# FP4 weights of the last block: transposing the block scales alone and rounding the values in the transposed layout

## The chip, the cores and the metric

The kernel runs on one core of a Trainium2 chip. The metric is the device time of one launch in microseconds, the median of several runs. TensorE is PE in the profile (its weight loads PEld), VectorE is DVE, ScalarE ACT, GpSimd POOL, and SyncE, which issues every DMA of this kernel, SP.

## The reference

A network of two gated blocks on x (8 batches of 224 rows, width 512), each made of a cross-attention to a context of 750 rows and a feed-forward part, both added with a tanh gate. Attention 0 has 16 heads of 32, attention 1 has 8 heads of 64 and a mask; feed-forward 0 is ternary with a depthwise convolution; feed-forward 1 is FP4. Only this last part matters here:

```python
def fp4_quant_dequant(x):            # BLOCK = 16, along the last dim
    xb = x.reshape(shape[:-1] + (shape[-1] // BLOCK, BLOCK))
    scale = jnp.max(jnp.abs(xb), axis=-1, keepdims=True) / 6.0
    scale = jnp.maximum(scale, jnp.float32(1e-12))
    xn = xb / scale
    idx = jnp.searchsorted(_MID, jnp.abs(xn))
    q = _GRID[idx] * jnp.sign(xn) * scale

def fp4_linear(x, w):
    return jnp.einsum('bsk,nk->bsn', fp4_quant_dequant(x), fp4_quant_dequant(w))

gate = fp4_linear(x, w_gate)
y = fp4_linear(x, w_up)
return fp4_linear(jax.nn.silu(gate) * y, w_down)
```

w_gate and w_up are 1408 x 512, w_down is 512 x 1408. A block is 16 neighbours along the contracted dimension, so a scale belongs to one output row and 16 inputs. TensorE wants the weights with the contracted dimension on the partitions, which is the transposed layout: there a block lies across 16 partitions.

## The kernel before, in words

The program is written as generators. Each yields pairs (PE us, DVE us) after handing out a few instructions; these are hints of cost, and the planner interleaves the generators by them. The order in which PE, DVE and ACT instructions are handed out is the order in which each engine runs them (`pin`). The order of SP and POOL is set when the program is built, by when each instruction is thought to be ready; each of them then works strictly in order.

There are 16 rounds of attention, n = 0 to 15: `attention16` for the 8 batches of block 0, then `attention8` (line 647 on) for those of block 1. A round of attention8 has 8 slots (4 head pairs, 2 row halves of 112). A slot does, on PE, the scores (L703), the product of the slot before with its values (L666), then other matmuls from queues, then the transposes of the softmax weights (L763). DVE adds the mask and takes the maximum (L720, L732), ACT takes the exponentials (L741) and copies the transposes out (L768). `fill` hands out matmuls of the queue (keys L312, queries L341, values L374, output projection L398) until a budget of PE us is spent; `pace` hands out steps of the list `beside` until a budget of DVE us is spent: 1.5 us ahead of the exponentials and 3.5 us in all by the second call in a slot. In slot 1 all values of the round are finished in one stretch (L374), and the next round's context is loaded (L293) once its buffer is free. L409 adds the output projection to x on DVE and so frees a bank of ps_m, of which there are two. L437, L439, L684 and L688 spread the softmax sums over the heads; they use the bank ps_t, of which there is one.

`last_weights` is the step in `beside` from round 8 on. It prepares the FP4 weights through `fp4_weights`, in 34 pieces of 128 rows by 512 (4 of them 384) columns: 11 of w_gate, 11 of w_up, 12 of w_down. For each piece:

- SP loads it (L1094, wraw), one piece ahead;
- `fp4_steps` finds the block maxima (L1061), the scale and its inverse (L1062, L1063), divides (L1066), rounds by adding and subtracting a power of two that is taken from the exponent (L1069, L1073 to L1075), and POOL multiplies by the scale again (L1076), in three steps with the hints 1.0, 1.1 and 1.6;
- one piece later PE transposes the 128 x 128 squares into ps_t (L1102, hint 0.45), four to a piece (three in a piece of 384), and ACT copies them to wg or wu (L1120), or to a buffer (L1130) from which SP writes them to the DRAM tensor wd_quantized (L1131).

Round 15 no longer has weights to prepare; its queue holds the first row tiles of feed-forward 1 (`ffn1_head`), which read wg and wu (L1168). After the attention `ffn1` runs the remaining tiles and loads wd once (L1316).

Of the kernel before, what the change touches and what calls it, by code (L numbers as in the profile page):

```python
# [63 lines left out]
class Net:  # L64
# [1014 lines left out]
    def fp4_weights(self, work, puts):  # L1079
# [5 lines left out]
            (put, src, r, c0, min(D, n_cols - c0))  # L1085
            for put, src, n_rows, n_cols in puts
# [4 lines left out]
        def load(n):  # L1091
            _, src, r, c0, width = pieces[n]
            raw = work.tile([128, D], F32, name="wraw", bufs=2)[:, :width]
            nc.sync.dma_start(out=raw, in_=src[r * 128 : (r + 1) * 128, c0 : c0 + width])  # L1094
            return raw

        def transposed(n, q):
            put, _, r, c0, width = pieces[n]
            nk = width // 128
            pt = self.ps("t", [128, nk, 128])  # L1100
            for k in range(nk):
                nc.tensor.transpose(pt[:, k, :], q[:, k * 128 : (k + 1) * 128], self.ident)  # L1102
            put(pt, c0 // 128, r)

        raw = load(0)
        for n in range(len(pieces)):
            ahead = load(n + 1) if n + 1 < len(pieces) else None
            q = work.tile([128, D], F32, name="wq4", bufs=2)[:, : pieces[n][-1]]
            yield from self.fp4_steps(work, q, raw, pieces[n][-1])
            if n:  # L1110
                transposed(n - 1, before)
                yield 0.45, 0
            raw, before = ahead, q
        transposed(len(pieces) - 1, q)

    def kept(self, dst):


        def put(pt, k, r):
            self.nc.scalar.copy(dst[:, k : k + pt.shape[1], r * 128 : (r + 1) * 128], pt)  # L1120

        return put

    def sent(self, work, dst):


        def put(pt, k, r):
            nk = pt.shape[1]
            some = work.tile([128, 4, 128], F32, name="wsome", bufs=2)
            self.nc.scalar.copy(some[:, :nk, :], pt)  # L1130
            self.nc.sync.dma_start(  # L1131
                out=dst[:, k : k + nk, r * 128 : (r + 1) * 128], in_=some[:, :nk, :]
            )

        return put
# [215 lines left out]
    def run(self):  # L1351
# [42 lines left out]
        def last_weights():  # L1394
# [5 lines left out]
            yield from self.fp4_weights(  # L1400
                self.ppool,
                (
                    (self.kept(self.wg), t["w_gate"], HID1, D),
# [153 lines left out]
```

## Time and profile before

| what | value |
|---|---|
| median of 3 runs | 2153.29 us (2151.72 to 2155.82) |
| the profiled execution, its own time | 2156.02 us |
| its span in the profile | 2154.2 us |
| first load of w_gate to last write of wd_quantized | 1171.6 to 1571.7 us |
| L1102, PE transposes of the weights | 132 of 273 ns |
| L1120 and L1130, copies to wg, wu and the send buffer | 34, of 585 ns (478 ns with 384 columns) |
| mean granted TensorE clock | 0.998 |

The time of a run is a little longer than the span, which is what the profiler saw of the engines. Times of single instructions below come from the profiled execution. A group of the profile is one line of the kernel on one engine: busy time, mean ns of one, then the idle time of the engine just ahead of it and what ended that. An instruction of PE is counted from its start to its modelled end; consecutive ones overlap, so what one costs in a row is read from the starts.

### The profile page before, as it was taken

The numbers are of one execution on the slowest core, as the hardware profiler recorded it, in microseconds if no ns is written. First come the engines' busy times: TensorE is split into PE (matmuls) and PEld (weight loads), VectorE is DVE, ScalarE is ACT, GpSimd is POOL, SyncE is SP. The second block draws the span as 40 slices with busy tenths as digits, with TensorE's granted clock in tenths as the row PEclk, the third lists the DMA queues.
The fourth block names the chain that finished last, engine by engine and source line by source line (L and its number), as shares of the span: only waits on it lengthen the run. The fifth ranks groups of instructions, "written<-read, shape, count | busy, mean of one in ns | idle before, by whom it ended". The sixth has DMA issues, their size and how long they took to land.

```text
span 2154.2 us, 32130 instructions
## 1 busy us (share of the span) xinstructions
PE 2107.8 (98%) x12606; PEld 1213.0 (56%) x12606; DVE 1362.9 (63%) x2795; ACT 1002.1 (47%) x2332; POOL 130.3 (6%) x146
## 2 busy tenths in 40 slices
PE   9999999999999999999999999999999999999999
PEld 5444545455554545455656575666656565665555
DVE  3776666677767676674456575654723467776665
ACT  3566667575767667573444343443534331111111
POOL 0000000000000000000000010111100001111111
PEclk9999999999999999999999999999999999999999
DMA  7200010100001010111011112112110011000000
GB/s 226 78 31 29 2 46 2 32 15 18 29 2 46 2 46 21 52 35 52 15 32 52 52 44 66 42 56 69 57 46 11 14 52 41 10 20 20 20 6 20
DMA packets 50215, 81.24 MB, mean 38 GB/s; under 512 B 3344, under 2 KB 29712, under 8 KB 49936
## 3 DMA queue, kind: packets, MB, share of 16 engines
q1 hardware_dynamic: 50064, 79.18, 11.7%
q8 instruction: 100, 1.64, 0.3%
q14 instruction: 51, 0.42, 0.1%
HBM read 65.28 MB, written 13.89 MB: 37 GB/s over the span
## 4 chain that ended last, share of the span: by engine, by line
PE 88%; DVE 5%; ACT 4%; issue 1%; DMA 0%; SPq 0%; POOL 0%; ACTq 0%; POOLq 0%; DVEq 0%
PE ps_m L374 15%; PE ps_m L312 13%; PE ps_big L1168 11%; PE ps_m L1200 6%; PE ps_pair L485 6%; PE ps_m L398 5%; PE ps_m L341 4%; PE ps_half L703 4%; PE ps_half L763 4%; PE ps_pa L666 4%; PE ps_pair L458 2%; ACT p L601 2%; PE ps_pa L576 2%; PE ps_t L907 2%; PE ps_m L1168 2%; PE ps_t L1021 1%
## 5 line engine op out<-in xcount | busy, mean ns | idle before, releaser
L502 ACT ACTIVATE p<-ps_pair,part 112x375 f32<-112x375 f32 x512 | 286.3, 571 | 192.0 <-DVE part L493 192.0
L312 PE MATMUL ps_m<-cx,wk 128*128 128x375 f32 x1024 | 370.5, 491 | 1.3 <-ACT kT L321 1.1
L374 PE MATMUL ps_m<-wv,cx 128*125 128x512 f32 x768 | 355.4, 602 | 0.0
L493 DVE TENSOR_REDUCE part<-ps_pair 112x2 f32<-112x750 f32 x256 | 228.2, 932 | 130.4 <-PE ps_pair L485 128.5
L312 PEld LDWEIGHTS ps_m<-cx,wk 128*128 128x128 f32 x1024 | 179.7, 191 | 118.0 <-issue 34.4
L374 PEld LDWEIGHTS ps_m<-wv,cx 128*125 128x125 f32 x768 | 135.5, 187 | 159.7 <-issue 158.0
L720 DVE CUSTOM_DVE_ANT_0 ps_half<-ps_half,mbias 112x750 f32<-112x750 f32 x128 | 121.1, 946 | 150.7 <-PE ps_half L703 150.0
L601 ACT ACTIVATE p<-ps_pair 125x896 f32<-125x896 f32 x192 | 165.0, 911 | 76.9 <-PE ps_pair L458 76.9
L485 PE MATMUL ps_pair<-kT,qT 32*112 32x375 f32 x1024 | 148.0, 522 | 0.2
L741 ACT ACTIVATE p<-ps_half,nm 112x750 f32<-112x750 f32 x128 | 113.4, 890 | 66.0 <-DVE nm L732 65.6
L1200 PE MATMUL ps_m<-wd,hqT 128*128 128x512 f32 x308 | 136.6, 592 | 0.0
L383 ACT COPY v<-ps_m 125x512 f32<-125x512 f32 x96 | 56.5, 589 | 152.2 <-PE ps_m L374 151.5
L935 DVE SCALAR_TENSOR_TENSOR y<-hp,cw,y 128x224 f32<-128x224 f32 x256 | 109.4, 448 | 20.2 <-ACT y L921 15.7
L398 PE MATMUL ps_m<-wo,aT 128*112 128x512 f32 x256 | 119.6, 602 | 0.0
L1179 ACT ACTIVATE gth<-ps_big 128x352 f32<-128x352 f32 x48 | 22.2, 463 | 206.9 <-PE ps_big L1168 206.9
L341 PE MATMUL ps_m<-xnT,wq 128*128 128x224 f32 x512 | 113.2, 360 | 0.6 <-ACT xnT L195 0.6
L1168 PE MATMUL ps_big<-wu,xqT 128*128 128x352 f32 x352 | 111.3, 459 | 0.0
L1168 PE MATMUL ps_big<-wg,xqT 128*128 128x352 f32 x352 | 111.3, 459 | 0.0
L768 ACT COPY p<-ps_half 125x672 f32<-125x672 f32 x128 | 85.9, 722 | 49.9 <-PE ps_half L763 49.7
L485 PEld LDWEIGHTS ps_pair<-kT,qT 32*112 32x112 f32 x1024 | 52.1, 170 | 98.7 <-ACT p L502 69.6
L502 ACT ACTIVATION_READ_ACCUMULATOR p<-ps_pair,part 112x1 f32 x512 | 103.5, 202 | 0.0
L763 PEld LDWEIGHTS ps_half<-ident,p 112*125 112x125 f32 x768 | 93.2, 189 | 16.1 <-issue 7.8
(223 smaller groups left out, 3026.4 us busy)
## 6 DMA issues: line engine op xcount, KB each, us to landing
cx<-in_ctx SPq DMA_DIRECT2D x32, 750.0 KB, 4.4
wst<-in_w SPq DMA_DIRECT2D x16, 512.0 KB, 8.1
x<-in_x SPq DMA_DIRECT2D x8, 448.0 KB, 6.0
mid<-x SPq DMA_DIRECT2D x8, 448.0 KB, 3.1
x<-mid SPq DMA_DIRECT2D x8, 448.0 KB, 3.5
last<-x SPq DMA_DIRECT2D x8, 448.0 KB, 3.1
out<-yout SPq DMA_DIRECT2D x14, 256.0 KB, 2.0
wraw<-in_w_gate SPq DMA_DIRECT2D x11, 256.0 KB, 2.6
```

The costliest lines, as they stand in the source:

```text
L312: nc.tensor.matmul(pk, lhsT=self.w["wk"][:, k, g * 128 : (g + 1) * 128], rhs=job["cx"][c][:, k, :], start=k == 0, stop=k == KC - 1,)
L341: nc.tensor.matmul(pq[:, g - g0, :], lhsT=self.w["wq"][:, k, g * 128 : (g + 1) * 128], rhs=xnT[:, k, :], start=k == 0, stop=k == KC - 1,)
L374: nc.tensor.matmul(pv, lhsT=job["cx"][c][:, k, at : at + CP], rhs=self.w["wv"][:, k, :], start=k == 0, stop=k == KC - 1,)
L398: nc.tensor.matmul(po, lhsT=aT[:, g, i * TP : (i + 1) * TP], rhs=self.w["wo"][:, g, :], start=g == 0, stop=g == KC - 1,)
L485: nc.tensor.matmul(sc[h // 2][:, h % 2, :MH], lhsT=qT[r, g, i * TP : (i + 1) * TP], rhs=kT[g][r, c * MH : (c + 1) * MH], start=True, stop= ...
L493: nc.vector.tensor_reduce(part[:, c, i, g, 2 * k : 2 * k + 2], sc[k][:, :, :MH], AX.X, ALU.max, negate=True)
L502: nc.scalar.activation(shown[:TP, h, :MH], sc[h // 2][:, h % 2, :MH], AF.Exp, bias=part[:, c, i, g, h : h + 1], accum_out=sums[:, c, i, g, ...
L601: nc.scalar.activation(p[:, 2 * k : 2 * k + 2, :], pw[k][:, :, : 2 * S], AF.Exp)
L720: nc.vector.tensor_tensor_reduce(out=src, in0=src, in1=masks[i], scale=1.0, scalar=-MASKED, op0=ALU.add, op1=ALU.max, accum_out=mx,)
L763: nc.tensor.transpose(pt[:, j // half, j % half * TP : (j % half + 1) * TP], p[:, h, j * CP : (j + 1) * CP], self.ident[:TP, :TP],)
L1168: nc.tensor.matmul(ps[:, :CW], lhsT=xqT[:, k, :], rhs=wt[:, k, c0 : c0 + CW], start=k == 0, stop=k == KC - 1,)
L1200: nc.tensor.matmul(po, lhsT=hqT[:, k, :], rhs=wd[:, k, :], start=k == 0, stop=k == NC1 - 1)
```

## The change

The values are no longer transposed on PE. The host hands in the three matrices in the transposed layout as well (w_gateT, w_upT, w_downT), beside the plain ones. The preparation has two passes for each matrix:

- `fp4_scales` (34 pieces as before) loads the plain piece, finds scale and inverse on DVE into one tile of 128 x 64 (wboth), transposes that tile with one PE instruction into ps_t, copies the 64 x 128 result to wrows (two buffers) on ACT, and writes it with two DMAs (scale, inverse; each from 32 partitions, 24 in a piece of 384) to a DRAM tensor, each row 16 times over, so that there every weight of the transposed layout has its own scale and inverse;
- `fp4_blocks` (35 pieces: 12 of w_gateT, 12 of w_upT, 11 of w_downT) loads a piece of the transposed matrix and the two pieces of scales and inverses that belong to it, divides and rounds on DVE with plain operands in place of broadcast ones, and POOL multiplies by the scale straight into wg or wu; for w_down it multiplies in place and SP writes the piece to wd_quantized.

The hints become 1.3 (scales), 0.1 for PE (its transpose), and 1.2 and 1.9 (values). wraw has three buffers instead of two. The order is: scales of w_gate, scales of w_up, values of w_gate, scales of w_down, values of w_up, values of w_down.

```diff
-    def fp4_weights(self, work, puts):
+    def fp4_scales(self, work, src, n_rows, n_cols, dst):
         nc = self.nc
         pieces = [
-            (put, src, r, c0, min(D, n_cols - c0))
-            for put, src, n_rows, n_cols in puts
+            (r, c0, min(D, n_cols - c0))
             for r in range(n_rows // 128)
             for c0 in range(0, n_cols, D)
         ]
         def load(n):
-            _, src, r, c0, width = pieces[n]
-            raw = work.tile([128, D], F32, name="wraw", bufs=2)[:, :width]
+            r, c0, width = pieces[n]
+            raw = work.tile([128, D], F32, name="wraw", bufs=3)[:, :width]
             nc.sync.dma_start(out=raw, in_=src[r * 128 : (r + 1) * 128, c0 : c0 + width])
             return raw
-        def transposed(n, q):
-            put, _, r, c0, width = pieces[n]
-            nk = width // 128
-            pt = self.ps("t", [128, nk, 128])
-            for k in range(nk):
-                nc.tensor.transpose(pt[:, k, :], q[:, k * 128 : (k + 1) * 128], self.ident)
-            put(pt, c0 // 128, r)
+        def sent(n, both):
+            r, c0, width = pieces[n]
+            nb = width // BLK
+            pt = self.ps("t", [2 * nb, 128])
+            nc.tensor.transpose(pt, both.rearrange("p a b -> p (a b)"), self.ident)
+            rows = work.tile([64, 128], F32, name="wrows", bufs=2)[: 2 * nb, :]
+            nc.scalar.copy(rows, pt)
+            for k in range(2):
+                nc.sync.dma_start(
+                    out=dst[k, c0 : c0 + width, r * 128 : (r + 1) * 128].rearrange(
+                        "(b j) n -> b j n", j=BLK
+                    ),
+                    in_=rows[k * nb : (k + 1) * nb, :].unsqueeze(1).to_broadcast([nb, BLK, 128]),
+                )
         raw = load(0)
-        for n in range(len(pieces)):
+        for n, (_, _, width) in enumerate(pieces):
             ahead = load(n + 1) if n + 1 < len(pieces) else None
-            q = work.tile([128, D], F32, name="wq4", bufs=2)[:, : pieces[n][-1]]
-            yield from self.fp4_steps(work, q, raw, pieces[n][-1])
+            nb = width // BLK
+            most = work.tile([128, D // BLK], F32, name="wmost", bufs=2)[:, :nb]
+            both = work.tile([128, 2 * D // BLK], F32, name="wboth", bufs=2)[:, : 2 * nb]
+            both = both.rearrange("p (a b) -> p a b", a=2)
+            nc.vector.tensor_reduce(
+                most, raw.rearrange("p (b k) -> p b k", k=BLK), AX.X, ALU.max,
+                apply_absolute_value=True,
+            )
+            nc.vector.tensor_scalar(both[:, 0, :], most, 1.0 / 6.0, 1e-12, ALU.mult, ALU.max)
+            nc.vector.reciprocal(both[:, 1, :], both[:, 0, :])
+            yield 0, 1.3
             if n:
-                transposed(n - 1, before)
-                yield 0.45, 0
-            raw, before = ahead, q
-        transposed(len(pieces) - 1, q)
-
-    def kept(self, dst):
-
-
-        def put(pt, k, r):
-            self.nc.scalar.copy(dst[:, k : k + pt.shape[1], r * 128 : (r + 1) * 128], pt)
-
-        return put
-
-    def sent(self, work, dst):
-
-
-        def put(pt, k, r):
-            nk = pt.shape[1]
-            some = work.tile([128, 4, 128], F32, name="wsome", bufs=2)
-            self.nc.scalar.copy(some[:, :nk, :], pt)
-            self.nc.sync.dma_start(
-                out=dst[:, k : k + nk, r * 128 : (r + 1) * 128], in_=some[:, :nk, :]
+                sent(n - 1, before)
+                yield 0.1, 0
+            raw, before = ahead, both
+        sent(len(pieces) - 1, both)
+        yield 0.1, 0
+
+    def fp4_blocks(self, work, src, scales, n_rows, n_cols, dst, kept):
+
+
+        nc = self.nc
+        pieces = [
+            (k, c0, min(D, n_cols - c0)) for k in range(n_rows // 128) for c0 in range(0, n_cols, D)
+        ]
+
+        def load(n):
+            k, c0, width = pieces[n]
+            rows, cols = slice(k * 128, (k + 1) * 128), slice(c0, c0 + width)
+            got = []
+            for name, ap in (
+                ("wraw", src[rows, cols]),
+                ("wscale", scales[0, rows, cols]),
+                ("winv", scales[1, rows, cols]),
+            ):
+                bufs = 3 if name == "wraw" else 2
+                got.append(work.tile([128, D], F32, name=name, bufs=bufs)[:, :width])
+                nc.sync.dma_start(out=got[-1], in_=ap)
+            return got
+
+        got = load(0)
+        for n, (k, c0, width) in enumerate(pieces):
+            ahead = load(n + 1) if n + 1 < len(pieces) else None
+            a, scale, e = got
+            nc.vector.scalar_tensor_tensor(a, a, DOWN, e, ALU.mult, ALU.mult)
+            nc.vector.tensor_scalar(
+                e.bitcast(I32), a.bitcast(I32), EXPONENT, None, ALU.bitwise_and
             )
-
-        return put
+            yield 0, 1.2
+            nc.vector.tensor_scalar(e, e, 1.0, STEP, ALU.max, ALU.mult)
+            nc.vector.tensor_tensor(a, a, e, ALU.add)
+            nc.vector.tensor_tensor(a, a, e, ALU.subtract)
+            where = dst[:, k, c0 : c0 + width]
+            nc.gpsimd.tensor_tensor(where if kept else a, a, scale, ALU.mult)
+            if not kept:
+                nc.sync.dma_start(out=where, in_=a)
+            yield 0, 1.9
+            got = ahead
     def ffn1_in(self, work, f, x, xn, xqT, bufs):
...
             self.wg = w1pool.tile([128, KC, HID1], F32, name="wg")
             self.wu = w1pool.tile([128, KC, HID1], F32, name="wu")
             self.ppool = self.pool(prep, "prep", side="left")
-            yield from self.fp4_weights(
-                self.ppool,
-                (
-                    (self.kept(self.wg), t["w_gate"], HID1, D),
-                    (self.kept(self.wu), t["w_up"], HID1, D),
-                    (self.sent(self.ppool, self.wd), t["w_down"], D, HID1),
-                ),
-            )
+            dram = self.pool(self.ctx, "scales", space=bass.MemoryType.DRAM)
+            sizes = {"w_gate": (HID1, D), "w_up": (HID1, D), "w_down": (D, HID1)}
+            scales = {
+                name: dram.tile([2, cols, rows], F32, name=f"scales_{name}")
+                for name, (rows, cols) in sizes.items()
+            }
+
+            def first(name):
+                return self.fp4_scales(self.ppool, t[name], *sizes[name], scales[name])
+
+            def second(name, dst, kept=True):
+                rows, cols = sizes[name]
+                src = t[name + "T"]
+                return self.fp4_blocks(self.ppool, src, scales[name], cols, rows, dst, kept)
+
+            yield from first("w_gate")
+            yield from first("w_up")
+            yield from second("w_gate", self.wg)
+            yield from first("w_down")
+            yield from second("w_up", self.wu)
+            yield from second("w_down", self.wd, False)
         rest, old = iter(()), []
         for n in range(2 * B):
...
         "w_gate": laid(L1_ffn_w_gate),
         "w_up": laid(L1_ffn_w_up),
         "w_down": laid(L1_ffn_w_down),
+        "w_gateT": laid(np.transpose(L1_ffn_w_gate)),
+        "w_upT": laid(np.transpose(L1_ffn_w_up)),
+        "w_downT": laid(np.transpose(L1_ffn_w_down)),
     }
     nc = bacc.Bacc("TRN2", target_bir_lowering=False, num_devices=1)
```

## The prediction, made before the run

> **What bounds the kernel now.** I read the page's busy line first, then a window table and the chain of waits cut to the stretch in which the FP4 weights are prepared, then the groups of that stretch with their shapes, then the timeline of one slot of attention8, and last the DMA view.
>
> ```profile
> PE 2107.8 (98%) x12606; PEld 1213.0 (56%) x12606; DVE 1362.9 (63%) x2795; ACT 1002.1 (47%) x2332; POOL 130.3 (6%) x146
> ...
> 1171.20:1571.80 400.60, 397.73 (x2433) 254.11 (x2432) 251.73 (x599) 171.35 (x334) 46.63 (x48) 1.00 0.19 57
> ...
> by line: PE ps_m L312 21.9%; PE ps_m L374 21.1%; PE ps_half L703 12.7%; PE ps_half L763 11.4%; PE ps_pa L666 11.4%; PE ps_m L341 7.6%; PE ps_m L398 6.9%; PE ps_t L1102 4.9%; PE ps_m L194 0.8%; PE ps_t L684 0.4%; ACT sT L439 0.4%; PE ps_t L4
> ```
>
> PE is busy 397.7 of these 400.6 us at full clock (1.00) and the chain runs on it, so what leaves PE's queue here should leave the time, and any new PE wait is added to it. L1102, the transposes that the change removes, is 4.9% of the chain: 19.6 us. DVE and ACT have room on average (252 and 171 us).
>
> ```profile
> L1102 PE MATMUL ps_t<-ident,wq 128*128 128x128 f32 x132 | 21.7, 286 | 2.9 <-ACT sT L439 2.1 <-ACT wsome L1130 0.8
> L1061 DVE TENSOR_REDUCE q_most<-wraw 128x32 f32<-128x512 f32 x30 | 20.3, 676 | 0.0
> L1066 DVE SCALAR_TENSOR_TENSOR q_a<-wraw,q_inv 128x512 f32<-128x512 f32 x30 | 20.8, 692 | 1.0
> L439 ACT COPY sT<-ps_t 128x224 bf16<-128x224 bf16 x8 | 2.8, 345 | 16.5 <-PE ps_t L437 16.5
> L1120 ACT COPY wg<-ps_t 128x512 f32<-128x512 f32 x11 | 6.4, 585 | 31.6 <-PE ps_t L1102 31.6
> ...
> 1240.29 0.66 PE L1102 MATMUL ps_t<-ident,wq 128*128 128x128 f32 x4
> 1240.78 2.69 PE L312 MATMUL ps_m<-cx,wk 128*128 128x375 f32 x8
> ...
> 1249.38 0.27 PE L437 MATMUL ps_t<-ident,stat 112*128 112x112 bf16 x2
> 1250.17 0.63 PE L1102 MATMUL ps_t<-ident,wq 128*128 128x128 f32 x4 [0.53 <-ACT sT L439]
> ```
>
> Four transposes take 0.49 us from their first start to the next matmul's, 0.123 each. The last pair of lines is the price of the single bank ps_t: when two of its users follow one another on PE, the second stands until ACT has emptied the bank, 0.53 us here. That happened 5 times (2.9 us).
>
> ```profile
> q1 hardware_dynamic: 50064, 79.18, 11.7%
> ...
> cx<-in_ctx SPq DMA_DIRECT2D x32, 750.0 KB, 4.4
> wraw<-in_w_down SPq DMA_DIRECT2D x8, 256.0 KB, 2.7
> wd_quantized<-wsome SPq DMA_DIRECT2D x8, 256.0 KB, 2.5
> ```
>
> 79.18 MB took 11.7% of 16 engines' 2154 us, so all 16 together move 314 GB/s and 256 KB occupy them 0.84 us.
>
> **Removed.** 132 transposes x 0.123 = 16.2 us, and their 2.9 us of waits: 19.1 us of PE time, near the chain's 19.6. The order of work has them between matmuls with nothing else to release, so I count all of it. The fill counts them at 0.45 us a piece, so slots keep their length by taking other matmuls earlier; the gain shows at the end of each batch, where fewer are left. ACT loses 34 copies of about 585 ns and gains 34 of about 265 (0.83 ns an element between the 224- and 512-element rows); it isn't the bound.
>
> **DVE and POOL.** Scales: 676+182+353 ns a piece (L1061 to L1063), as before. Values: 692+427+426+692+692 ns; the operands are plain instead of broadcast, and I take the same time, since L1066 with its broadcast takes what L1074 without takes. Over 35 pieces holding the same elements, DVE's sum is unchanged. The slot's mix is not: 3 scale pieces (3.6 us) or 1.5 value pieces (4.4) against one piece (4.1) before, beside 2.5 us of L720 and L732. The matmuls of a slot last about 9.1 us (L703 starts at 1237.6 and 1246.6), so this hides at zero; uncovered, 0.3 us x some 24 slots, 7 us. POOL's multiply moves to wg and wu: same 1.08 us, off the path. That the cost hints rise (3.7 to 4.4 us a piece) only spreads the work; it still ends before the last batch.
>
> **Added on PE.** 34 transposes, one a piece: 34 x 0.123 = 4.2 us.
>
> **Added waits on ps_t.** Scale pieces come three to a slot, two of them back to back. In the built order 16 of the 34 have another user of ps_t straight ahead (13 a scale transpose, 3 an L437). Start to start by the row above: transpose 0.27, 0.04, copy 0.27, 0.14: 0.72 instead of 0.12, so 0.6 us each. For 14 of them 8.4 us; the two others are dearer. Behind the waiting transpose stands all of PE. Bounds: 0.45 each (6.3) to 0.9 (12.6), if ACT is busy.
>
> **Added waits through wrows and SP.** wrows has two buffers, so a piece's copy waits on ACT until the two writes of two pieces earlier have landed. The nearest row is wd_quantized<-wsome, 256 KB also in 512-byte rows, 2.5 us. With t the start of a transpose: copied at t+0.6, SP issues at 0.7 and 1.1, landed at 0.7+2.5+0.84 = t+4.0. At the ends of w_gate and w_up, four transposes come as two pairs with 1.8 us of matmuls between; the fourth needs the third's copy, which waits for the first's landing: it starts at t+4.5, not 2.7, 1.8 us each, plus 0.6 where a 750 KB context load is ahead in the queue: 4.2 us. L684 in one slot behind such a copy: 0.5. Scale work of the same slot not yet done on DVE (first slot 0.6, one other 0.3, last piece of w_down 1.0): 1.9. In the other slots ACT is held from t+2.9 to t+4 or 5; its next urgent work, L768, is due about t+4.5, and the raw loads share the engines: I take 0.2 x 10 = 2 (bounds 0 and 8).
>
> **The transition from w_down's scales to w_up's values.** SP runs in order, so the first w_upT load stands behind the last scale writes (issued about t+4.8): landed about t+8.6. The first value step (1.1 us) waits for it on DVE, and L409 (0.75), which frees a ps_m bank, is queued behind it, done at t+10.5. PE wants that bank at about t+8.2 (three transposes with their waits 2.6, two L398 1.7, two L312 1.3, L763 1.3, two L312 1.3): 2.3 us (bounds 0 and 5). Elsewhere value loads run one piece ahead, about 3.5 us against 5.4 us between a buffer's release and its use; nothing there, 1 us x 8 if the context loads get between.
>
> **Added DMA.** 68 writes and 70 scale reads of 256 KB or less and about 34 raw loads: 172 x 0.84 = 144 us of engine time in some 400, where the share was 0.19: covered. SP issues cost 0.34 to 0.38 us each; SP is idle otherwise. Behind blocked issues stand the context, mask and x loads; each has more than 10 us before its use. But in a scale slot it is 9 x 0.84 = 7.5 us of 9.1, and here a rule speaks against the change. The nearest row reads 128 partitions. The Trainium skill (SBUF — State Buffer, section "Door 1: The DMA port swizzle") says that partitions 0 to 63 reach only half of the DMA ports: 189 GB/s from 32 partitions against 328 from 128, at 1 MiB. The scale writes read 32 partitions each. By the row a write occupies 0.84 us; by the rule an estimate of 0.84 x 328/189 = 1.46, the slot 6 x 1.46 + 3 x 0.84 = 11.3 us, above 9.1. No row here reads few partitions. I take the row, as it has the same bytes, packets and direction, and keep the rule as a rival.
>
> **Sum.** -19.1 + 4.2 + 8.4 + 4.2 + 0.5 + 1.9 + 2.0 + 2.3 = +4.4 us. On the profiled execution's own 2156.0 (span 2154.2) that is 2160.4; it lies 2.7 above the median of 2153.3, and on the median the forecast is 2157.7. About 0.2% (4.3 us) is what a measurement can tell from no change. So: slower by a hair, the PE time saved being paid back in waits for a bank and for buffers.
>
> **Rivals.**
> 1. Not slower (chance 0.2): the writes out of wrows land before the buffer is wanted again, in the bursts and at the transition, so that nothing of the 10.9 us of the last five terms reaches PE and only the bank waits remain: -19.1+4.2+8.4 = -6.5, 2146.8. For it speaks that PE waited only 2.9 us on ACT in this stretch; against, that two buffers and one bank leave no slack in a burst of four. It decides once more than 4.4 of the 10.9 us vanish.
> 2. Clearly slower (0.2): the port rule holds. A scale slot is then bound by the write queue: 11.3-9.1 = 2.2 us x 9 slots = 20 us less 4 taken up by the long stretch of values: +16 on the forecast, 2174. Against it: the row.
> 3. The PE time isn't worth what it says (0.1): slots paced by DVE or ACT, so that neither saving nor waits count: 2153.
>
> The first case (0.5) covers 2150 to 2166: faster 0.03, same 0.20, slower 0.27. Rival 1: faster 0.19, same 0.01. Rival 2: slower 0.20. Rival 3: same 0.08, slower 0.02. Together faster 0.22, same 0.29, slower 0.49. The range goes from rival 1's middle, 2146, to rival 2's, 2174.
>
> **What would show it.** L1100 with 34 transposes and idle before it of 10 to 16 us, released by ACT wrows; ACT's wrows copy waiting on DMA; scale writes landing at 2.5 to 3.5 us (rival 2: 5 and more, DMA share near 1 in scale slots); L409 late once; slots with value pieces without PE waits. Wrong I am if L720 starts late in value slots and p L741 holds PE's L763, or if PE's idle stays under 5 us.

## The result, and the profile after

The changed kernel takes 2180.74 us (median of 4 runs, 2177.52 to 2182.10) against 2153.72 us of the kernel before beside it (2151.72 to 2155.82): ratio 1.0123, 95% interval 1.0106 to 1.0141. It is 27 us slower. The forecast was 2157.7 with a range of 2146 to 2174, so the sign was right and the time lies outside the range. The profiled execution took 2182.1 us, its span is 2180.3.

From the page of the changed kernel: the busy line, the granted clock in 40 slices of 54.5 us, the hardware queue, and the landing time of one group of scale writes.

```profile
PE 2110.5 (97%) x12508; PEld 1206.4 (55%) x12508; DVE 1380.4 (63%) x2800; ACT 992.1 (46%) x2332; POOL 147.0 (7%) x147
...
PEclk9999999999999999999999989999999999999999
...
q1 hardware_dynamic: 95792, 122.45, 19.1%
...
scales_w_gate<-wrows SPq DMA_DIRECT2D x22, 256.0 KB, 4.8
```

PE issues 98 instructions less than before and is busy 2.7 us *longer*; the clock row, all nines before, has an eight in one slice (from 1254 to 1308 us). The scale writes of w_gate land after 4.8 us, those of the other two after 4.2 (medians of the landings that the trace could place, 9 of 68); I had taken 2.5, from the row wd_quantized<-wsome.

The window table of the changed kernel: the same 400.6 us as shown of before, then the slots behind the long stretch of the round in which w_up's scales end and w_gate's values begin, then the last round with weights, in which only values are left.

```profile
1171.20:1571.80 400.60, 375.56 (x2144) 227.81 (x2143) 229.71 (x537) 150.86 (x313) 48.31 (x38) 0.97 0.54 146
1237.95:1319.85 81.90, 72.33 (x449) 47.79 (x448) 50.41 (x123) 32.64 (x70) 8.72 (x7) 0.92 0.65 165
1513.57:1603.84 90.27, 89.88 (x529) 55.56 (x528) 64.14 (x130) 35.81 (x70) 17.61 (x15) 1.00 0.43 139
```

Against 397.73 busy of 400.60 at full clock before, PE now stands 25 us and runs at a granted clock of 0.97 (the share of its full clock that PE was given). The second row is where most is lost: 9.6 of 81.9 us idle, clock 0.92, and the DMA engines busy for 0.65 of the time (0.19 before, over the 400.6 us). The third row is the other half of the change: PE busy 89.88 of 90.27 us, full clock. A whole round of before took 93.2 us. Read from the starts of L703, the rounds of the changed kernel are 112.7, 93.4, 100.4, 90.3 and 91.3 us long, those of before 93.3, 93.3, 93.2, 94.3 and 92.2. So the loss is +5.2 us ahead of the first of these rounds, +19.4 in the first, +7.2 in the third; the rounds with values alone are 4 us and 1 us *shorter*. Those with the loss are the ends of w_gate's and w_up's scales and the change from w_down's scales to w_up's values, the places that the prediction named.

The groups of the stretch, after:

```profile
L1118 DVE TENSOR_REDUCE wmost<-wraw 128x32 f32<-128x512 f32 (+1 forms) x34 | 22.0, 647 | 28.0 <-DMA wraw<-in_w_up 14.8 <-DMA wraw<-in_w_down 6.7 <-DMA wraw<-in_w_gate 6.5
...
L1100 PE MATMUL ps_t<-ident,wboth 128*64 128x128 f32 (+1 forms) x34 | 10.4, 305 | 16.0 <-DVE wboth L1123 8.4 <-ACT wrows L1102 6.7 <-ACT sT L439 0.9
...
L1102 ACT COPY wrows<-ps_t 64x128 f32<-64x128 f32 (+1 forms) x34 | 8.8, 258 | 60.2 <-PE ps_t L1100 33.5 <-DMA scales_w_gate<-wrows 9.0 <-DMA scales_w_down<-wrows 8.2
```

L1100 has its 34 transposes, and 16.0 us of waits ahead of them, at the upper end of the 10 to 16 foreseen. But the releaser is not the one foreseen: more than half is DVE's wboth L1123, and the first row says why: DVE's L1118 stood 28.0 us for the *loads* of the raw weights, which before never made it wait (L1061: 0.0). ACT's copy waits for the landing of earlier writes as foreseen (23.2 us in the waits of three tensors, of which the row shows two).

The timeline at the end of w_up's scales shows the chain of causes in one place:

```profile
1279.56 0.27 PE L1100 MATMUL ps_t<-ident,wboth 128*64 128x128 f32 x1
...
1279.81 7.87 SPq L1104 DMA_DIRECT2D scales_w_up<-wrows  x6
...
1282.35 0.26 ACT L1102 COPY wrows<-ps_t 64x128 f32<-64x128 f32 x1 [1.69 <-DMA scales_w_up<-wrows]
1283.11 0.69 DVE L1118 TENSOR_REDUCE wmost<-wraw 128x32 f32<-128x512 f32 x1 [3.70 <-DMA wraw<-in_w_up]
...
1284.62 0.39 PE L1100 MATMUL ps_t<-ident,wboth 128*64 128x128 f32 x1 [4.79 <-DVE wboth L1123]
...
1286.83 2.70 PE L763 MATMUL ps_half<-ident,p 112*125 112x112 f32 x12
```

SP spends 7.87 us on six writes: 5.76 us issuing them, 0.55 to 1.46 us each (the nearest row of before, L1131, took 0.37 us for one), and the rest standing until ACT's copies, themselves waiting for landings, have filled the next rows. The raw load that was issued just ahead of them (at 1278.77) lands late, DVE's reduce starts at 1283.11 after 3.70 us of waiting, the next transpose at 1284.62 after 4.79. Then a further loss: the twelve L763 take 2.70 us. In a slot of before they took 1.46:

```profile
1271.03 1.46 PE L763 MATMUL ps_half<-ident,p 112*125 112x112 f32 x12
```

The clock had fallen with the stall: in the 5.5 us from 1284.6 on it was granted at 0.50.

### The profile page after: what moved, and what is told of

It reads as the page before. It is cut to its first block, busy times and chain, and to the rows that moved or that the text cites. A ratio compares the mean times of both kernels' runs of the same rounds, so it can differ in the third digit from the quotient of the medians.

```text
span 2180.3 us, 32257 instructions
## 1 busy us (share of the span) xinstructions
PE 2110.5 (97%) x12508; PEld 1206.4 (55%) x12508; DVE 1380.4 (63%) x2800; ACT 992.1 (46%) x2332; POOL 147.0 (7%) x147
## 3 DMA queue, kind: packets, MB, share of 16 engines
q1 hardware_dynamic: 95792, 122.45, 19.1%
## 4 chain that ended last, share of the span: by engine, by line
PE 84%; DVE 7%; ACT 5%; DMA 2%; issue 1%; SPq 1%; POOL 0%; ACTq 0%; DVEq 0%; POOLq 0%
PE ps_m L374 15%; PE ps_m L312 12%; PE ps_big L1204 10%; PE ps_m L1236 6%; PE ps_pair L485 6%; PE ps_m L398 5%; PE ps_m L341 4%; PE ps_half L703 4%; PE ps_half L763 4%; PE ps_pa L666 3%; PE ps_pair L458 2%; ACT p L601 2%; PE ps_pa L576 2%; PE ps_t L907 2%; PE ps_m L1204 2%; PE ps_t L1021 1%
## 5 line engine op out<-in xcount | busy, mean ns | idle before, releaser
L312 PE MATMUL ps_m<-cx,wk 128*128 128x375 f32 x1024 | 376.9, 496 | 2.9 <-ACT kT L321 2.2
L720 DVE CUSTOM_DVE_ANT_0 ps_half<-ps_half,mbias 112x750 f32<-112x750 f32 x128 | 121.1, 946 | 141.9 <-PE ps_half L703 141.2
L741 ACT ACTIVATE p<-ps_half,nm 112x750 f32<-112x750 f32 x128 | 113.3, 887 | 128.4 <-DVE nm L732 128.1
L935 DVE SCALAR_TENSOR_TENSOR y<-hp,cw,y 128x224 f32<-128x224 f32 x256 | 109.5, 448 | 20.3 <-ACT y L921 15.8
L763 PEld LDWEIGHTS ps_half<-ident,p 112*125 112x125 f32 x768 | 94.9, 192 | 18.9 <-ACT p L741 7.1
```

The source lines that it names most:

```text
L312: nc.tensor.matmul(pk, lhsT=self.w["wk"][:, k, g * 128 : (g + 1) * 128], rhs=job["cx"][c][:, k, :], start=k == 0, stop=k == KC - 1,)
L720: nc.vector.tensor_tensor_reduce(out=src, in0=src, in1=masks[i], scale=1.0, scalar=-MASKED, op0=ALU.add, op1=ALU.max, accum_out=mx,)
L763: nc.tensor.transpose(pt[:, j // half, j % half * TP : (j % half + 1) * TP], p[:, h, j * CP : (j + 1) * CP], self.ident[:TP, :TP],)
```

## The experiments

Theory 1: the scale writes, read from few neighbouring partitions, are too slow for a slot with three scale pieces; all of the loss follows from that. Theory 2: the value pass costs the time. Theory 3: the hand-over of one bank and two buffers costs it, whatever the speed of the writes. Times of the kernel before in the three sets of experiments were 2155.06, 2153.72 and 2154.00 us; each ratio is to the one beside it. It is not the quotient of the two medians, from which it differs by up to 0.1%.

| kernel | us | ratio to before, 95% interval |
|---|---|---|
| changed | 2180.74 | 1.0123 (1.0106 to 1.0141) |
| values only | 2138.54 | 0.9927 (0.9910 to 0.9943) |
| half of the scale writes | 2157.79 | 1.0013 (1.0006 to 1.0020) |
| small scale writes | 2157.54 | 1.0017 (1.0011 to 1.0024) |
| spread over slots | 2154.66 | 1.0001 (0.9993 to 1.0010) |
| small and spread over slots | 2147.77 | 0.9966 (0.9955 to 0.9978) |
| the same, two pieces a transpose | 2145.73 | 0.9960 (0.9946 to 0.9974) |
| more buffers | 2175.20 | 1.0096 (1.0081 to 1.0111) |
| writes from POOL's queue | 2185.59 | 1.0149 (1.0134 to 1.0164) |
| 64 source partitions, every second | 2162.80 | 1.0035 (1.0022 to 1.0048) |
| 32, every fourth | 2171.94 | 1.0081 (1.0066 to 1.0096) |
| 64 neighbours | 2168.60 | 1.0060 (1.0044 to 1.0075) |
| multiply on DVE | 2181.48 | 1.0126 (1.0111 to 1.0141) |

**Values only.** The scale pass is left out, and the value pass reads weights in place of scales.

```diff
-            yield from first("w_gate")
-            yield from first("w_up")
             yield from second("w_gate", self.wg)
-            yield from first("w_down")
             yield from second("w_up", self.wu)
...
-                ("wscale", scales[0, rows, cols]),
-                ("winv", scales[1, rows, cols]),
+                ("wscale", src[rows, cols]),
+                ("winv", src[rows, cols]),
```

> Leaves the whole scale pass out (no reduce, no small transposes, no wrows copies, no 256 KB scale writes); the value pass reads the weights themselves where it would read scales and inverses, so it still moves the same bytes and does the same DVE and POOL work on wrong numbers. Theory 1 (the scale writes are too slow for their slots, and everything lost is lost in the scale slots): PE has 132 transposes less than the kernel before and no waits, so about 2153.7 - 19.1 = 2135 us (2130 to 2140), with no slot of attention8 longer than 10 us outside the long stretch. Theory 2 (the value pass loses the time, by DVE and POOL getting in each other's way: L1159 takes 1.1 us where 0.43 was expected): the value slots keep their length, 2160 us or more.

2138.54 us. One round of it in the window table:

```profile
1290.01:1379.67 89.66, 89.66 (x530) 55.58 (x529) 62.37 (x131) 35.90 (x70) 17.53 (x15) 1.00 0.40 123
```

PE is never idle, with the whole value pass beside it. Theory 2 falls: the value pass costs nothing, and the change without its scales gains 16.5 us. The loss is 42.2 us (2180.74 - 2138.54), and all of it goes with the scale pass.

**Half of the scale writes.** Only the scales are written; the inverses are left out.

```diff
-            for k in range(2):
+            for k in range(1):
...
-                ("winv", scales[1, rows, cols]),
+                ("winv", scales[0, rows, cols]),
```

> Writes only the scales, not their inverses (one 256 KB write a piece instead of two); the value pass reads the scales twice. PE, ACT and DVE have the same instructions and buffers. Theory 1 (rate of the scale writes): a slot with three scale pieces then has 3 writes of about 1.3 us instead of 6, well below its 9.1 us; most of the loss goes: 2150 to 2158 us, idle before L1100 under 20 us instead of 42. Theory 3 (the hand-over of the one bank ps_t and of two wrows buffers costs the time whatever the writes' rate): 2170 us or more, since a copy still has to wait for a landing.

2157.79 us, idle before L1100 11.0 us. Half the bytes take away 23 of the 42 us. The remaining writes still land only after 3.3 to 4.0 us, so it isn't the latency of one write that costs the 23, but how many of them follow one another.

**Small scale writes.** Each row is written once; the repetition is done by the loads.

```diff
-                    out=dst[k, c0 : c0 + width, r * 128 : (r + 1) * 128].rearrange(
-                        "(b j) n -> b j n", j=BLK
-                    ),
-                    in_=rows[k * nb : (k + 1) * nb, :].unsqueeze(1).to_broadcast([nb, BLK, 128]),
+                    out=dst[k, c0 // BLK : c0 // BLK + nb, r * 128 : (r + 1) * 128],
+                    in_=rows[k * nb : (k + 1) * nb, :],
...
-                ("wscale", scales[0, rows, cols]),
-                ("winv", scales[1, rows, cols]),
+                ("wscale", scales[0, k * 8 : k * 8 + 8, cols]),
+                ("winv", scales[1, k * 8 : k * 8 + 8, cols]),
...
+                if name != "wraw":
+                    ap = ap.unsqueeze(1).to_broadcast([8, BLK, width])
```

> Each scale row is written to DRAM once (two writes of 16 KB a piece instead of 256 KB), and the value pass's loads repeat each row for its 16 partitions as they read. PE, ACT and DVE have the same instructions, buffers and bank as in the changed kernel. Theory 1: nothing is left of the write queue; what stays over the kernel without a scale pass (2138.5) are 34 transposes, 4.2 us, and waits on the one bank of at most 8.4 us: 2142 to 2151 us. Theory 3 (hand-over whatever the rate): a small write takes about 2 us to land too, so the waits on wrows stay at half: 2156 to 2164 us. If a load that repeats a row out of DRAM is slow, wscale and winv land late (over 4 us), and the value slots get waits that they don't have now.

2157.54 us, above the 2142 to 2151 of theory 1 and in theory 3's reach at its lower end. With the writes' bytes gone, 19.0 us of the scale pass stay. The group of transposes:

```profile
L1100 PE MATMUL ps_t<-ident,wboth 128*64 128x128 f32 (+1 forms) x34 | 10.0, 295 | 10.1 <-ACT wrows L1102 6.0 <-DVE wboth L1121 2.8 <-ACT sT L439 1.3
```

34 x 0.123 = 4.2 us are work, 10.1 us these waits, 1.5 those of L684 behind such a copy: 15.8 of the 19.0. The waits are on the bank (ACT, which empties it) and on DVE; on landings of the small writes ACT's copies wait 1.5 us in sum, and 2.6 us more in one wait that the trace puts down to a load. The two times, with half of the written bytes and with a sixteenth, are the same (2157.79 and 2157.54): from half the bytes down their size costs nothing more, and the other half costs 23 us.

**Spread over slots**, first with the full writes, then with the small ones.

```diff
             nc.vector.reciprocal(both[:, 1, :], both[:, 0, :])
-            yield 0, 1.3
+            yield 0, 2.6
```

> Only the planner's hint of a scale piece is raised from 1.3 to 2.6 us, so that one or two scale pieces come to a slot instead of three; same work, same bytes, spread over about twice as many slots. Theory 1: two or four writes of about 1.3 us in a slot of 9.1 leave room; waits before the small transposes under 8 us: 2144 to 2152 us, less than the kernel before. Theory 3: each copy of a pair still waits for a landing, half of the hand-overs stay: 2158 to 2166 us.

> The small writes of the run before and the hint of 2.6 us together. If the bank's waits come only from small transposes that follow one another, they go as well: 2141 to 2146 us, the fastest of all versions with the whole work. If it equals the run with the small writes alone within 2 us, back-to-back transposes cost next to nothing by themselves.

With the full writes 2154.66, above theory 1's 2144 to 2152; with the small ones 2147.77, above the 2141 to 2146 expected. Both fall far below the 2180.74, with the same transposes, bank and buffers: what is dear is three pieces in a slot. The group in the second kernel:

```profile
L1100 PE MATMUL ps_t<-ident,wboth 128*64 128x128 f32 (+1 forms) x34 | 9.8, 289 | 3.7 <-ACT sT L439 2.2 <-ACT wrows L1102 1.5
```

10.1 us of waits have become 3.7: the bank's cost was that of transposes directly behind one another. Of the 6.9 us between the two kernels, 6.6 come from a single slot of 15.83 us (9.22 with the small writes), shown by the first one's timeline:

```profile
1260.12 0.69 DVE L1118 TENSOR_REDUCE wmost<-wraw 128x32 f32<-128x512 f32 x1 [8.21 <-DMA wraw<-in_w_up]
...
1263.23 2.13 PE L666 MATMUL ps_pa<-p,v 125*64 125x112 f32 x20 [3.70 <-DVE aT L692]
```

A raw load stands behind the writes, DVE's reduce waits 8.21 us for it, and L692, queued behind that on DVE, is late for PE. The mechanism of the changed kernel, once instead of in a row of slots.

**More buffers.** The rows go into quarters of two larger tiles, up to eight pieces between copy and reuse; wboth has four buffers.

```diff
-            rows = work.tile([64, 128], F32, name="wrows", bufs=2)[: 2 * nb, :]
+            if n % 4 == 0:
+                store.append(work.tile([128, D], F32, name="winv", bufs=2))
+            rows = store[-1][: 2 * nb, n % 4 * 128 :][:, :128]
```

> The transposed rows go into 4 quarters of each of two 2 KB tiles (up to 8 pieces between a copy and the reuse of its place instead of 2), and wboth has 4 buffers instead of 2; same transfers, same one bank. Theory 3 (it is the hand-over of two buffers): no copy waits for a landing any more, the waits before the small transposes shrink to those on the bank: 2150 to 2156 us. Theory 1 (rate of the writes): six writes still fill a slot's transfer time and the raw loads stand behind them, so DVE's reduce comes late; a part of the loss goes, 2160 to 2172 us, and wmost's wait on wraw stays above 15 us.

2175.20 us, a little less of a gain than theory 1 gave (2160 to 2172), and far from theory 3's 2150 to 2156. The waits of ACT's copy on landings fall to 4.0 us, while wmost's on wraw are 39.7. ACT no longer waits for the writes, but DVE waits longer for the loads that are queued with them. Theory 3 explains 5.5 of the 42 us here.

**Writes from POOL's queue.** `nc.sync.dma_start` becomes `nc.gpsimd.dma_start` for the scale writes.

> The scale writes are issued from POOL's queue instead of SP's; nothing else changes. Theory 1c (the loss is mostly head-of-line: raw loads stand behind blocked writes in SP's queue, so DVE's reduce and with it the next transposes come late): raw loads land in 2.6 us again, the waits of wmost on wraw (28 us in three tensors) go, and the time falls to 2160 to 2168 us. If instead the transfers themselves are the limit, the engines are shared in the same way and the wrows copies wait as before: 2176 us or more.

2185.59 us, no faster than the changed kernel, where 2160 to 2168 had been expected if the order in SP's queue were the cause. That order is real, and not the whole: DVE no longer waits for raw loads at all (0.0 us before L1118 instead of 28.0), but ACT's copies now wait 42.0 us for landings instead of 23.2. The writes land after 5 us on a queue of their own, and the raw loads of w_up after 5.1 us instead of 4.4. What all of them share is the transfer itself. The edit is not quite a clean one: in POOL's queue the writes go in packets of some 3.2 KB (17.31 MB in 5440) instead of 512 bytes.

**Which property of the source makes a write slow.** Three kernels hold every scale row twice, in 128 partitions. The first reads 64 partitions, every second one, each row 8 times:

```diff
-            rows = work.tile([64, 128], F32, name="wrows", bufs=2)[: 2 * nb, :]
+            rows = work.tile([128, 128], F32, name="wrows", bufs=2)[: 4 * nb, :]
...
-                        "(b j) n -> b j n", j=BLK
+                        "(b j) n -> b j n", j=BLK // 2
-                    in_=rows[k * nb : (k + 1) * nb, :].unsqueeze(1).to_broadcast([nb, BLK, 128]),
+                    in_=rows[k::2, :].unsqueeze(1).to_broadcast([2 * nb, BLK // 2, 128]),
```

The second reads `rows[k::4, :]`, 32 partitions, each row 16 times as in the changed kernel. The third keeps the two copies of the scales in the lower half of the rows and those of the inverses in the upper one, and reads 64 neighbours, each row 8 times. All three do somewhat more work on DVE and PE than the changed kernel, because the tiles are twice as wide.

> Same bytes, but each write reads 64 partitions spread over all 128 (every scale row is there twice, each copy is written 8 times) instead of 32 neighbouring ones 16 times. Theory 1a (few source partitions make a write slow): writes land in 2.5 to 3.3 us instead of 4.2 to 4.8, and the time falls to 2155 to 2162 us. Theory 1b (the writes are slow for another reason: 512-byte packets to DRAM at this stride, or the same row read again and again): they land in 4 us or more as before, and the time stays at 2177 to 2183 us.

> As in the run with 64 spread partitions every scale row is in the buffer twice, but each write reads only one copy: 32 partitions, every fourth one, each row written 16 times as in the changed kernel. Theory 1a' (where the source partitions lie decides): as fast as with 64 spread ones, landing about 3.0 to 3.4 us, q1's share 18.2 to 18.5%, 2159 to 2166 us. Theory 1a'' (how many partitions are read, or how often each row is read again): landing 4 us or more, q1's share 19% or more, 2172 us or more.

> The counterpart: each write reads 64 partitions, each row 8 times, but they are neighbours: scales from partitions 0 to 63, inverses from 64 to 127. Theory 1a' (where they lie): each write by itself is slow again, landing 4 us or more, 2170 us or more; if the two halves help one another because the two writes overlap, up to half of it may go (2166). Theory 1a'' (how many, how often): as with 64 spread ones, 3.0 to 3.4 us, 2159 to 2165 us.

64 spread ones: landing 3.0 to 3.3 us, 2162.80, just above the 2155 to 2162 of theory 1a. 32 spread ones: landing 3.3 to 3.4 and a queue share of 18.4%, both as place would have it, but a time of 2171.94, at the edge of what number or repetition would have. 64 neighbours: landing 3.9 to 4.0, share 19.0%, 2168.60, between the two. The landings speak for the place, the times for both: at an equal number of partitions and of repetitions the spread source takes 8.8 us (32) or 5.8 us (64) less than the neighbours, but 64 also take some 9 to 12 us less than 32. So the writes were run alone, 22 of 256 KB back to back in each form, in one run without any other work of the kernel:

> Only DMA writes, no other work of the kernel (the output is zeros): stages of 22 writes of 256 KB back to back into a tensor laid out like the scales of w_gate, 512-byte rows, one stage after the other, which differ only in the source: 32 neighbouring partitions each row 16 times (as in the changed kernel), 32 spread ones 16 times, two halves of 64 neighbours in turn 8 times, 64 neighbours of the lower half for all 8 times, 64 spread ones 8 times, all 128 4 times, all 128 without repetition; at the end 11 raw loads. If where the partitions lie decides: about 1.2 to 1.4 us a write for neighbours 32 and 64 lower, 0.8 to 0.9 for all spread forms and for 128, the two halves in turn between. If the number of partitions or of repetitions counts by itself: 32 spread slower than 64 spread by 0.2 us or more, which would explain why 32 spread ones left the kernel at 2171.9 us and 64 at 2162.8 with the same packet times.

SP's timeline in that kernel; the second column is the time in which SP issued the 22 writes, which is that of the transfers, because SP is held up by them. The order is 32 neighbours, 32 spread, two halves in turn, 64 neighbours of the lower half, 64 spread, 128 with each row 4 times, 128 plain. The raw loads, meant for the end, came between the stages.

```profile
10.79 28.97 SPq L1403 DMA_DIRECT2D to_near<-rows  x22
...
44.37 19.66 SPq L1403 DMA_DIRECT2D to_spread<-rows  x22
...
67.66 22.48 SPq L1403 DMA_DIRECT2D to_halves<-rows  x22
...
93.69 26.88 SPq L1403 DMA_DIRECT2D to_lower<-rows  x22
124.68 19.01 SPq L1403 DMA_DIRECT2D to_spread<-rows  x22
147.30 19.04 SPq L1403 DMA_DIRECT2D to_all<-rows  x22
170.19 18.84 SPq L1421 DMA_DIRECT2D to_plain<-rows  x22
```

Divided by 22: 1.32 us a write from 32 neighbours, 1.22 from 64, 0.86 to 0.89 from all spread forms and from 128 partitions, whether rows are repeated 16 times or not at all, and 1.02 when two halves take turns. The first six stages write to tensors of the same layout in the same 512-byte packets, so it isn't the target. For the rate alone, where the source partitions lie decides; their number and the repetition count for little (0.10 us between 32 and 64 neighbours, 0.03 between 32 and 64 spread ones). The 0.84 us that the prediction took is right for the row that it came from (0.86 here), and wrong for these writes by 0.48 us. The kernel with 32 spread partitions is 9 us slower than the one with 64, at nearly the same rate alone. Their two traces show what these microseconds are: 4.0 us more of PE standing (60.7 against 56.7) and 6.7 us more of PE busy on the same instructions (2111.2 against 2104.5) at a mean clock of 0.994 against 0.998. The longest stall of PE, at the end of w_up's scales, is 3.95 us with 32, ended by DVE, which had waited 2.67 us for a raw load, and 1.43 us at that place with 64; the clock falls only behind the longer one. Why the raw load is late with 32 stays open.

**Multiply on DVE.** `nc.gpsimd.tensor_tensor` becomes `nc.vector.tensor_tensor` in the value pass.

> The changed kernel with the value pass's last multiply on DVE instead of POOL. If DVE's L1159 (1.0 us on average where 0.43 was expected) is long because POOL's multiply of the piece before works at the same time, it falls to 0.43 us. DVE does 35 x 0.69 = 24 us more and gets 35 x about 0.55 = 19 back. If the value slots cost the time nothing, as theory 1 has it, the time stays at 2176 to 2185 us; if the value pass has a share in the loss, the time changes by 5 us or more.

2181.48 us, the same; what it shows of the engines stands in the last section.

**Two pieces in one transpose.** On top of small and spread: two pieces' scales and inverses lie side by side in one tile of 128 columns, with one transpose and one copy for both.

```diff
+            at = batch[-1][-1] if batch else 0
+            batch.append((pieces[n], at, at + 2 * nb))
+            here = both[:, at : at + 2 * nb].rearrange("p (a b) -> p a b", a=2)
...
+            nc.tensor.transpose(pt, both[:, : batch[-1][-1]], self.ident)
```

> The version with small writes and the hint of 2.6 us, with two pieces put in one transpose (128 columns instead of 64): 18 or 19 transposes and copies instead of 34. If what is left over the kernel without a scale pass (9.2 us) goes with the number of transposes (0.123 us each, and a bank wait for some), about half of it goes: 2142 to 2145 us. If it stays at 2147 to 2149, the rest is something else than the transposes.

2145.73 us, 2.0 less than with 34 transposes, between the two expectations: 16 transposes less at 0.123 are 2.0 us, and the waits hardly changed (2.9 us before the transposes, 3.7 with 34). The intervals of the two ratios overlap, so the step is not clear of noise. By its median it is the fastest kernel with the whole work, 0.40% below the kernel before (0.26 to 0.54%).

## Why the prediction was wrong

**Removed, -19.1:** right within the error, near its edge. Without the scale pass the change gains 16.5 us (interval 12.3 to 19.4).

**DVE and POOL of the value pass, nothing:** right for the time, wrong in the rows. L1159 was taken at 427 ns and takes 1000, POOL's multiply at 1.08 us and takes 1.26 to 1.65 for most pieces of full width; the rounds with values show no PE wait from them.

**Added on PE, +4.2, and waits on ps_t, +8.4:** right. With small writes, where nothing else is left, the waits on the bank are 7.3 us (6.0 + 1.3), those on DVE 2.8 (taken: 1.9), L684's 1.5 (0.5). The kernel gives 19.0 us for the scale pass; some 3 us of that have no row of their own.

**wrows and SP, 4.2 and 2.0:** right in the place, wrong in the size. The prediction had the fourth transpose of a burst 1.8 us late. It came 2.93 us late at the end of w_gate, released by ACT's copy as foreseen, and 4.79 us at the end of w_up, this time by a way that was not in the sum: late raw loads, which hold DVE.

**The transition from w_down, +2.3:** right in the place. The first value step waited for its load. But it did not reach PE through L409 as the prediction said; these three lines of the changed kernel's timeline show the way:

```profile
1454.19 0.69 DVE L1158 SCALAR_TENSOR_TENSOR wraw<-wraw,winv 128x512 f32<-128x512 f32 x1 [10.01 <-DMA wraw<-in_w_upT]
...
1460.87 0.89 ACT L741 ACTIVATE p<-ps_half,nm 112x750 f32<-112x750 f32 x1 [8.81 <-DVE nm L732]
...
1461.90 0.91 PE L763 MATMUL ps_half<-ident,p 112*125 112x112 f32 x6 [2.78 <-ACT p L741]
```

DVE is held by L1158 for 10.01 us, so L720 and L732 come late, ACT's L741 with them, and PE waits 2.78 us at L763: what the prediction had listed as a sign that it was wrong. The slot took 14.58 us, where undisturbed ones take some 9.3; the whole round is the one with +7.2 us.

**Added DMA: this is the step that failed.** It priced a scale write at 0.84 us, called the sum covered, and put nothing down for what a full queue delays: "I take the row, as it has the same bytes, packets and direction, and keep the rule as a rival." The row reads 128 partitions; the writes read 32 neighbours and take 1.32 us alone. By that rate, and as an estimate, a slot with three pieces needs 6 x 1.32 + 3 x 0.84 = 10.4 us of 9.1, where 7.5 was taken. With half the writes it is 3 x 1.32 + 3 x 0.84 = 6.5. What the experiments show is the price of the writes: 2180.74 - 2157.54 = 23.2 us go when they are small, 23.0 when half of them are left out, and 26.1 when the full ones are spread over more slots (where the waits on the bank are fewer as well). In the two profiled spans, of the changed kernel and of the one with small writes, those are 14.8 us more of PE standing (69.8 against 55.0) and 9.7 us more of PE busy on the same 12508 instructions, the latter at a lower clock (0.995 against 0.998; 0.50 behind the longest stall). Both mechanisms, raw loads that come late and hold DVE, and the clock, were priced at nothing.

The wrong rate is only a part of the 23.2 us. With the source spread, and so at 0.89 or 0.86 us a write, the estimate for a slot is 7.9 or 7.7 us of 9.1, yet these kernels take 2171.94 and 2162.80: the spread source gives back 8.8 us with 32 partitions and 17.9 with 64, and 5.3 us stay even then. So the fit of a slot is a sign and not a price. That the kernel with small writes meets the forecast (2157.54 against 2157.7) is in part luck: the forecast had 8.5 us of waits for landings (4.2 + 2.0 + 2.3) that this kernel hardly has, 2.6 us more of saving than was measured, and less of the other waits than it has.

The rule that was kept as a rival (the Trainium skill, "SBUF — State Buffer", section "Door 1: The DMA port swizzle": a transfer's rate depends on how many of the SBUF's ports its partitions reach, and partitions 0 to 63 reach no more than 0 to 31) is what the writes alone show: 199 GB/s from 32 neighbours (256 KB in 1.32 us), 215 from 64, 305 from 128. Its estimate of 1.46 us a write was 0.14 too high, and rival 2's 2174 still 7 us too low: it counted the excess of the queue, but neither the late raw loads nor the clock, whose shares in these 7 us no run separates. Rival 1's condition, no waiting for landings, held in the kernel with small writes, and gave 2157.5 instead of 2146.8: the waits on DVE and on the bank stay.

## What to carry to other kernels

Take a transfer's price from a row with the same *source and target partitions*, not only with the same bytes and packets; where no row has them and a rule speaks, put the rule's price into the sum of the fullest slot and see whether it still fits. A slot that fits on average can still be late in a burst, as the spread sources showed. When a queue no longer fits into its slot, what comes late is everything else in that queue: count the loads behind it, the engine that waits for them, what is queued behind that engine's waiting instruction, and the clock after the stall. And where a row has to be repeated, try to let the DMA that reads it back repeat it: here that made a 256 KB write 16 KB, and with the pieces spread over more slots the change became faster than the kernel before.

## What the runs showed of the hardware

- **Place of the source.** 22 writes of 256 KB back to back took 28.97 us from 32 neighbouring partitions and 19.66 from 32 spread over all 128, as fast within 5% as from all 128 (18.84 to 19.04). Two halves in turn took 22.48, so writes from different halves do help one another somewhat.
- **SP is held by its queue.** In the row of 22 writes from 32 neighbours the first two issues took SP 0.68 and 0.65 us and the median one 1.34, the pace of the transfers. In the changed kernel an issue of such a write took 0.55 to 1.85 us, and a load behind it waits for it.
- **The clock behind a stall.** After a stall of 4.79 us the next twelve L763 took 2.70 us instead of 1.46, at a granted clock of 0.50 for 5.5 us. Shorter stalls did it too: behind that of 2.93 us the clock was 0.50 for 3.4 us, and so it was in the kernel with small writes behind one of 1.50 us, while one of 1.88 us in the kernel with half of the writes left it at full. So the length of a single stall does not tell it. In the kernel without the scale pass, where PE never stood longer than 0.32 us while the weights were prepared, the mean was 1.000.
- **DVE and POOL in each other's way.** The first line is of the changed kernel, the second of the one with the multiply on DVE; the mean of one is the number after the busy time.

```profile
L1159 DVE TENSOR_SCALAR winv<-wraw 128x512 int32<-128x512 int32 x27 | 27.0, 1000 | 0.9
```

```profile
L1159 DVE TENSOR_SCALAR winv<-wraw 128x512 int32<-128x512 int32 x27 | 12.0, 445 | 0.9
```

The same instruction takes 1000 ns on average with the multiply on POOL and 445 with it on DVE, and the multiply takes 692 ns on DVE against 1.26 to 1.65 us for most on POOL. The single instructions say more than the mean: 9 of the 27 run while POOL is idle and take 427 ns; the other 18 start beside a multiply and take 1.10 to 1.39 us, and each of them ends 0.28 to 0.29 us after that multiply. The Trainium skill's "SBUF — State Buffer" (section "🔬 SBUF: two separate sides") has the two engines share a pair of ports that one holds for a whole instruction; these ends agree. It cost no time here, because DVE had room.
